# Attention, convolution and MLP layers on one core: where the convolution's taps stand in the attention, and which block goes first

## The chip, the cores and the metric

The kernel runs on one core of a Trainium2 chip, with all arithmetic in fp32. The metric is the device time of the execution in microseconds (us), the median of several runs. A profile, taken by the hardware from a further execution, gives every instruction of every engine: TensorE (PE, with weight loads as PEld), VectorE (DVE), ScalarE (ACT), GpSimd (POOL) and SyncE (SP), which issues the transfers (DMA).

## The reference

Four layers follow each other on x of 16 images, 384 channels, 16 x 16 pixels. Cut to what matters:

```
# layer 0: attention over 8 frames x 256 pixels (N = 2048 tokens), 12 heads of 32, batch of 2
q, k = xt @ qk_w.T ;  v = xt
attn = alpha * eye + beta * softmax(q k^T / sqrt(32)) - gamma / N
x = attn @ v
# layer 1: depthwise 7x7, LayerNorm over channels, MLP 384 -> 1536 -> 384
y = LN(conv7x7(x)) ; h = gelu(y @ w1 + b1)
h = grn_g * h * norm(h) / mean(norm(h)) + grn_b + h      # response normalization
x = x + h @ w2 + b2
# layer 2: x + gelu(LN(fusion_w @ [sobel_x(x), sobel_y(x)]))
# layer 3: 1x1, depthwise 3x3, 1x1 (with residual); linear attention; LN and MLP (with residual)
```

Layer 0 needs all tokens of a batch element. From layer 1 on, two images (512 columns) can be worked on by themselves.

## The kernel before

**Tiling.** Channels lie on partitions in three chunks of 128. The 2048 tokens of a batch element are four blocks of 512 columns; with two batch elements there are eight blocks, named here by (batch, block): (0, 0) is the first, (0, 1) the second.

**Attention (`attention`, L411).** The outer loop has six units (batch element, channel chunk of four heads), each with four blocks of queries, each with 16 steps over keys (`NQC` = 16). So there are 24 blocks of 16 steps, counted t = 0 to 383. A step has four score products (`st`) on TensorE, four exponentials (`e`) on ScalarE, and, a step later, four products with the values (`av`). The denominator needs the sum of e over all keys. VectorE adds the e of several steps into `s` (2048 elements a partition), and TensorE multiplies the group's sum with ones (`dn`). `ADDS` has the group size for each block: 16 means 15 sums on VectorE and one dn at the end; 4 means 12 sums, and the first three groups go to TensorE in four parts each. At a block's end a `finish` sends the denominator through DRAM twice (`away`, `few`, `back`, `r`) so that its reciprocal is cheap, and scales the result (`va`, `l`). Projections of q and k for the coming blocks (`p`) stand at the head of each block as long as there are any; the last stand at t = 320 and t = 336.

**Work put into the attention.** The attention's instructions are issued in a fixed order on PE, ACT and DVE (`InOrder`, L91). At each step `fill` (L1521) may put in operations of layer 1: the taps of the 7x7 convolution (`convolutions`, L906: per chunk one ScalarE pass and 48 multiply-adds on VectorE, rows y<-l,vec,y), and the *leads*, the normalization of the first two blocks (`layer1`, L1052). `pace` (L199) gives, for a step, how long TensorE is taken to need and how much VectorE has to do; the difference, less what was owed before (`lag`), is `free`. A VectorE operation is put in while `free` covers it. `FIRST` and `LEAD` are the first steps at which taps and leads may start. An operation that needs another ScalarE table (the square root of the normalization) is put in only ahead of a projection. Chunks listed together in `todo` alternate their taps; a chunk by itself runs its taps one after another, each dependent on the last. A chunk can start when the attention has finished that chunk of channels. The first matmul of the MLP waits for weights, and so can't stand in the attention.

**After the attention.** A planner (`Plan.all`, L185) orders all other operations from costs: at each turn it takes, of the operations that could start within `SLACK` of the earliest, the one whose task has the lowest rank (`RANK`: `mid` is layers 2 and 3 up to the linear attention, `l1` layer 1, `l3c` the last MLP, `conv` the remaining taps). `plan.level` (L1582) has VectorE begin 8 us and ScalarE 5 us after TensorE. `TURNS` is the order in which blocks use the MLP weights: each group loads its weights once and its first half may start only when the one before is through. `AFTER` says which block must have gone through layer 3's attention before the convolution of later blocks takes its tiles. Nearly every instruction is recorded with line L101, the helper that fixes the order, so the profile is read by the names of tiles: `ph_l` and `po_l` are the first and second product of layer 1's MLP, `ph_l3c` and `po_l3c` of the last, `su`, `sv` the products with ones for mean and variance, `s_l` their work tiles, `pg_l` the response normalization's, `pf_l` and `pc_l3a` those of layers 2 and 3.

Of the kernel before, what the change touches and what calls it, by code (L numbers as in the profile page):

```python
# [30 lines left out]
NIP = NBLK  # L31
NQC = N // P
PAIRED = (NB * NC - 1) * NBLK + 1
LEAD = 20 * NQC + 6
FIRST = NQC + 10

TURNS = (
# [1 line left out]
    (1, ((0, 0),)),  # L39
    (0, ((0, 3),)),  # L40
    (1, ((0, 1),)),
    (0, ((1, 0), (1, 1),)),
    (1, ((0, 2),)),
    (0, ((1, 3),)),
    (1, ((0, 3),)),
    (0, ((1, 2),)),
    (1, ((1, 1), (1, 0), (1, 3), (1, 2),)),
)
AFTER = ('x4', 0, 1)

RANK = {
    "mid": ((32.4, 40.6, 83.5, 47.6), (47.3, 49.0, 49.8, 34.6)),
    "l1": ((19.3, 43.7, 53.1, 86.8), (70.6, 16.2, 22.5, 90.5)),
    "l3c": ((87.9, 30.5, 79.2, 72.6), (54.9, 50.0, 67.3, 77.0)),
    "conv": 110.8,
}
SLACK = 0.191
JUNK = 2

ADDS = (16, 4, 16, 8, 8, 8, 16, 16, 4, 16, 8, 16, 4, 16, 8, 16, 16, 4, 16, 16, 16, 8, 16, 4)  # L60
XB, YB, SB = 12, 2, 22
TB = BLK // P
RB = 2 * HW
# [135 lines left out]
def pace(t):  # L199


    n, i = divmod(t - 1, NQC)
    adds = ADDS[n]
    pe, dve = 2.075, 2.2 if t and i % adds else 0.0
    parts = sum(
        min(k + 2 + j * adds // 4, NQC - 1) == i
        for k in range(adds - 1, NQC - 1, adds)
        for j in range(4)
    )
    pe += 0.21 * parts  # L210
    if i == adds + 1 and parts:
        pe += 0.15
    if t and i == NQC - 1 and n < PAIRED:
        pe += 1.1
    elif i == 1 and n > PAIRED:
        pe += 1.67
    elif not parts and adds < NQC and i > adds:
        pe += 0.09
    if n > 0:
        dve += {2: 0.17, 6: 0.6, 7: 0.66}.get(  # L220
            i - 2 * (n > PAIRED), 0.0
        )
    return pe, dve


class Task:
# [184 lines left out]
def attention(tc, X, xt, L0, block, small, col, cols, ones, load_qk, banks, fill, bound):  # L411
# [6 lines left out]
    with ExitStack() as actx:  # L418
# [50 lines left out]
        def unit(u, made, gm):  # L469

            b, g = units[u]
            q, keys, v = made["q"], made["k"], made["v"]
            adds = ADDS[u * NBLK : (u + 1) * NBLK]
            acc = {}
# [170 lines left out]
def conv_seq_kernel(  # L645
# [25 lines left out]
    def block(name, tag="x"):  # L671
        return blocks.tile([P, NC, BLK], F32, tag=tag, name=name, bufs=XB if tag == "x" else YB)
# [28 lines left out]
    def col(name, c, k=0):  # L701
        at, n = _COL[name]
        return vec[:, at + c * n + k : at + c * n + k + 1]
# [42 lines left out]
    pe, act, dve = (InOrder(tc, e) for e in (nc.tensor, nc.scalar, nc.vector))  # L746
# [149 lines left out]
    def together(*parts):  # L896

        parts = [[next(p), p] for p in parts]
        while parts:
            for p in list(parts):  # L900
                yield p[0]
                p[0] = next(p[1], None)
                if p[0] is None:
                    parts.remove(p)

    def convolutions():  # L906

        todo = [[(0, 0, 0)], [(0, 1, 0)], [(0, 0, 1)], [(0, 0, 2), (0, 1, 1)], [(0, 1, 2)]]
        todo += [[(b, i, c) for c in range(NC)] for b in range(NB) for i in range(NBLK)][YB:]
        for chunks in todo:  # L910
            for b, i, c in chunks:
                if c == 0:
                    tag = "y" if b == 0 or i < YB else "x"
                    after = [] if tag == "y" else [AFTER]
                    yield Op(None, 0.0, after=after, takes=[(tag, 1)], lag=0.0)
                    Y[b, i] = block(f"y_{b}_{i}", tag)
            yield from together(
                *(
                    depthwise(
                        Y[b, i][:, c, :],  # L920
                        L0[b][i][:, c, :],
                        lambda k, c=c: col("L1_dw_w", c, k),
                        col("L1_dw_b", c),
                        7,
                        ("y", b, i, c),
                        after=[("l0", b, i, c)],
                    )
                    for b, i, c in chunks
                )
            )  # L930
# [565 lines left out]

    bias = Task("bias", 0, fusion_bias())
    conv = Task("conv", RANK["conv"], convolutions())

    def rank(kind, b, i):  # L1500
# [12 lines left out]
    leads = [next(t for t in tasks if t.name == f"l1_0_{i}") for i in range(YB)]  # L1513

    if fast:
        open_pool("s", SB)
        open_pool("tiny", 2)

        lag = 0.0

        def fill(t, added=0.0):  # L1521


            nonlocal lag
            if t < 0:
                while plan.step(bias):
                    pass
                return
            if added is None:
                for task in leads:  # L1530
                    if task.head.table:
                        plan.step(task)
                return
            if t % NQC == 9 and t > NQC:
                u, i = divmod(t // NQC - 1, NBLK)
                plan.mark(("l0", u // NC, i, u % NC))
            length, work = pace(t)
            free = length + added - work - lag
            for task in (*leads, conv):
                if task.rest > t or t < (FIRST if task is conv else LEAD):  # L1540
                    continue
                before = None
                while task is not conv or ("y", 0, YB - 1, NC - 1) not in plan.made:
                    op = task.head
                    if op.table:
                        break
                    if before and before.engine != op.engine:
                        task.rest = t + 1 + (before.engine == "DVE")
                        break
                    if op.engine == "DVE":  # L1550
                        bank = any(tag == "mm" for tag, _ in op.gives)
                        if free < max(0.4, op.length - 1.5) and not bank:
                            break
                        free -= op.length + 0.12 * (before in op.after)
                    if not plan.holds(task, "wa") or not plan.step(task):
                        break
                    if op.engine in ("ACT", "PE"):
                        before = op
                        if task.head.engine == "ACT" and task is not conv:
                            task.rest = t + 1  # L1560
                            break
                    elif op.engine:
                        before = op
            lag = max(0.0, -free)

        attention(
            tc, X, xt, L0, block, small, col, cols, ones, first_loads, banks, fill, bound
        )
    else:
        attention_general(tc, X, L0, block, col, cols, ident, first_loads)  # L1570
        open_pool("s", SB)
        open_pool("tiny", 2)
# [33 lines left out]
    if fast:  # L1606
        tasks.append(Task("safety", 99, safety()))
    plan.all(tasks, SLACK)

# [90 lines left out]
```

## Time and profile before

| what | value |
|---|---|
| median of 3 runs | 2685.53 us (2685.33 to 2685.53) |
| the profiled execution's own time | 2687.06 us |
| its span, first to last instruction | 2685.1 us |
| PE busy | 2621.9 us (98%) |
| DVE busy | 2016.1 us (75%) |
| ACT busy | 1603.2 us (60%) |
| POOL busy | 7.5 us |
| granted TensorE clock, mean | 0.991 |
| end of the attention's last product on PE | 1033.5 us |
| DMA | 81.32 MB, 10% of the engines' time at most of the span |

The page has the span in 40 slices of 67.1 us, with a digit per slice for the busy tenths of each engine. A group's row has the operation, output <- input by the program's names, partitions x elements, the count, then busy time and mean of one, then the idle time before it and what ended it. A matmul in fp32 is recorded as two instructions, so that 72 rows of `po_l` are 36 products. A row in order of time has start, length, operation, and in brackets how long the engine had been idle before it and which operation ended that. In the slices 0 to 15 the attention runs, from slice 16 on the layers behind it.

### The profile page before, as it was taken

How to read it: one execution, taken by the hardware profiler on the slowest of the kernel's cores; microseconds unless marked ns; L12 is line 12 of the kernel's file. 1: busy time of each engine (PE TensorE's matmuls, PEld its weight loads, DVE VectorE, ACT ScalarE, POOL GpSimd, SP SyncE). 2: the span in 40 equal slices, each digit the busy share in tenths (PEclk: the TensorE clock that was granted, in tenths of full speed). 3: DMA queues.
4: the chain of work that ended last, by engine and by line, in shares of the span. 5: the costliest groups of instructions: out<-in, count | busy, mean ns of one | idle time of the engine just before them, and what ended most of it. 6: DMA issues, size and time to landing. Idle time of an engine off the chain costs nothing. (4 is left out here: it accounts for less than half of the span.)

```text
span 2685.1 us, 30687 instructions
## 1 busy us (share of the span) xinstructions
PE 2621.9 (98%) x11845; PEld 1026.3 (38%) x11845; DVE 2016.1 (75%) x2249; ACT 1603.2 (60%) x3083; POOL 7.5 (0%) x54
## 2 busy tenths in 40 slices
PE   9999999999999996899999999999999999999999
PEld 2222222222232222344444454445444544454443
DVE  5899999999999997999999899999653032542210
ACT  6888888888888895563554463654336644333220
POOL 0000000000000000000000000000000000000000
PEclk9999999999999998899999999999999999999999
DMA  3000000000000004000111112010110112000000
GB/s 142 18 9 21 6 17 17 9 21 6 17 17 5 9 17 138 0 1 0 36 36 36 53 57 79 24 36 12 36 59 24 35 59 94 12 1 12 1 12 25
DMA packets 51691, 81.32 MB, mean 30 GB/s; under 512 B 10608, under 2 KB 29168, under 8 KB 51536
## 3 DMA queue, kind: packets, MB, share of 16 engines
q1 hardware_dynamic: 51392, 79.12, 9.3%
q8 instruction: 95, 1.56, 0.2%
q14 instruction: 60, 0.49, 0.1%
q10 hardware_dynamic: 144, 0.15, 0.0%
HBM read 72.57 MB, written 6.68 MB: 30 GB/s over the span
## 5 line engine op out<-in xcount | busy, mean ns | idle before, releaser
L101 ACT ACTIVATE e<-st 128x512 f32<-128x512 f32 x1536 | 792.2, 611 | 56.3 <-PE st L101 36.7
L101 DVE TENSOR_TENSOR s<-s,e 128x2048 f32<-128x2048 f32 x294 | 673.6, 2291 | 26.9 <-ACT e L101 3.6
L101 DVE SCALAR_TENSOR_TENSOR y<-l,vec,y 128x420 f32<-128x420 f32 (+8 forms) x1152 | 660.6, 633 | 7.6 <-ACT y L101 1.4
L101 PE MATMUL st<-q,k 32*128 32x512 f32 x3072 | 451.2, 642 | 1.6 <-DVE y L101 1.3
L101 PE MATMUL av<-e,v 128*32 128x512 f32 x3072 | 437.2, 606 | 0.0
L101 PE MATMUL ph_l<-y,wa 128*128 128x512 f32 x576 | 260.4, 596 | 20.3 <-ACT y L101 20.3
L101 PE MATMUL po_l<-hid_l,wb 128*128 128x512 f32 x576 | 260.8, 601 | 2.3 <-ACT hid_l L101 2.2
L101 PE MATMUL ph_l3c<-d_l3c,wa 128*128 128x512 f32 x576 | 259.6, 595 | 0.0
L101 PE MATMUL po_l3c<-hid_l3c,wb 128*128 128x512 f32 x576 | 256.3, 593 | 0.0
L101 PEld LDWEIGHTS st<-q,k 32*128 32x128 f32 x3072 | 128.9, 183 | 285.2 <-issue 251.3
L101 PEld LDWEIGHTS av<-e,v 128*32 128x32 f32 x3072 | 79.8, 108 | 300.2 <-issue 274.5
L101 ACT ACTIVATE hid_l3c<-ph_l3c,vec 128x512 f32<-128x512 f32 x96 | 65.8, 686 | 190.2 <-PE ph_l3c L101 189.8
L101 ACT ACTIVATE hid_l<-ph_l,vec 128x512 f32<-128x512 f32 x96 | 65.8, 686 | 175.7 <-PE ph_l L101 175.6
L101 PEld LDWEIGHTS ph_l<-y,wa 128*128 128x128 f32 x576 | 109.6, 191 | 158.1 <-issue 126.8
L101 PEld LDWEIGHTS po_l<-hid_l,wb 128*128 128x128 f32 x576 | 109.2, 192 | 137.1 <-issue 122.9
L101 PEld LDWEIGHTS po_l3c<-hid_l3c,wb 128*128 128x128 f32 x576 | 109.0, 190 | 135.3 <-issue 133.2
L101 PEld LDWEIGHTS ph_l3c<-d_l3c,wa 128*128 128x128 f32 x576 | 108.1, 190 | 136.1 <-issue 129.5
L101 DVE SCALAR_TENSOR_TENSOR o_l3c<-po_l3c,vec,l 128x512 f32<-128x512 f32 x24 | 17.9, 748 | 187.4 <-PE po_l3c L101 186.6
L101 DVE SCALAR_TENSOR_TENSOR g_l3a<-h_l3a,dw,g_l3a 128x450 f32<-128x450 f32 (+1 forms) x192 | 119.2, 694 | 19.8 <-ACT g_l3a L101 19.7
L101 PE MATMUL p<-x,wqk_sb 128*128 128x512 f32 x288 | 131.2, 606 | 1.2 <-DMA x<-in_x_dram 1.2
L101 DVE TENSOR_TENSOR s<-e,e 128x2048 f32<-128x2048 f32 x45 | 102.9, 2286 | 35.1 <-ACT e L101 32.1
L101 ACT ACT_TABLE_LOAD x88 | 112.9, 1283 | 8.2 <-PE ph_l L101 4.5
(155 smaller groups left out, 2224.0 us busy)
## 6 DMA issues: line engine op xcount, KB each, us to landing
wa<-in_w_dram SPq DMA_DIRECT2D x15, 768.0 KB, 4.6
wb<-in_w_dram SPq DMA_DIRECT2D x15, 768.0 KB, 4.4
wa<-in_mlp_w_dram SPq DMA_DIRECT2D x15, 768.0 KB, 4.4
wb<-in_mlp_w_dram SPq DMA_DIRECT2D x15, 768.0 KB, 4.4
x<-in_x_dram SPq DMA_DIRECT2D x8, 768.0 KB, 9.3
v<-in_xt_dram SPq DMA_DIRECT2D x24, 256.0 KB, 10.7
r<-back SPq DMA_DIRECT2D x96, 64.0 KB, 2.1
out_dram<-o_l3c SPq DMA_DIRECT2D x24, 256.0 KB, 2.3
```

Of the source, the lines that this page charges most:

```text
L101: self.last = self.tc.keep_in_program_order(make(*args, **kw))
```

## The change

Four things are changed in the order of the work; no operation is added to the computation or left out.

- `pace` has other step lengths: 2.125 us for a step of TensorE in place of 2.075, 3.6 us for a block's last step, 0.16 us for a part of a group's dn.
- A tap is put in when `free` is at least 0.4 us and when VectorE, by `pace`, will not lag by more than 2.5 us at any step up to the block's end (new function `ahead`). Before, an operation needed `free` of its length less 1.5 us, and at least 0.4.
- The first block's second chunk in `todo` no longer alternates with the second block's: (0, 0, 2) stands by itself, then (0, 1, 1) and (0, 1, 2) alternate. The first block's lead may start at t = 294, the second's at 326 as before.
- `ADDS`, `TURNS`, `AFTER`, `RANK` and `SLACK` have other values.

```diff
-LEAD = 20 * NQC + 6
+LEAD = (18 * NQC + 6, 20 * NQC + 6)
...
-    (0, ((1, 0), (1, 1),)),
-    (1, ((0, 2),)),
-    (0, ((1, 3),)),
-    (1, ((0, 3),)),
-    (0, ((1, 2),)),
+    (0, ((1, 0),)),
+    (1, ((0, 2), (0, 3),)),
+    (0, ((1, 1), (1, 3), (1, 2),)),
     (1, ((1, 1), (1, 0), (1, 3), (1, 2),)),
 )
-AFTER = ('x4', 0, 1)
+AFTER = ('x4', 0, 2)
...
-    "mid": ((32.4, 40.6, 83.5, 47.6), (47.3, 49.0, 49.8, 34.6)),
-    "l1": ((19.3, 43.7, 53.1, 86.8), (70.6, 16.2, 22.5, 90.5)),
-    "l3c": ((87.9, 30.5, 79.2, 72.6), (54.9, 50.0, 67.3, 77.0)),
-    "conv": 110.8,
+    "mid": ((-10.7, 39.8, 15.4, 29.4), (92.4, 85.3, 93.3, 89.6)),
+    "l1": ((22.3, 22.5, 52.0, 45.4), (57.2, 52.1, 90.7, 8.2)),
+    "l3c": ((79.3, 2.7, 59.3, 70.1), (66.1, 61.4, 69.0, 118.4)),
+    "conv": 80.5,
 }
-SLACK = 0.191
+SLACK = 0.122
...
-ADDS = (16, 4, 16, 8, 8, 8, 16, 16, 4, 16, 8, 16, 4, 16, 8, 16, 16, 4, 16, 16, 16, 8, 16, 4)
+ADDS = (16, 8, 8, 16, 16, 16, 8, 8, 8, 4, 8, 8, 16, 4, 8, 4, 8, 8, 4, 8, 16, 16, 16, 16)
...
-    pe, dve = 2.075, 2.2 if t and i % adds else 0.0
+    pe, dve = 2.125, 2.2 if t and i % adds else 0.0
...
-    pe += 0.21 * parts
-    if i == adds + 1 and parts:
-        pe += 0.15
     if t and i == NQC - 1 and n < PAIRED:
-        pe += 1.1
+        pe = 3.6
     elif i == 1 and n > PAIRED:
         pe += 1.67
-    elif not parts and adds < NQC and i > adds:
-        pe += 0.09
+    elif parts:
+        pe += 0.16 * parts + 0.2 * (i == adds + 1)
...
+def ahead(t):
+
+    worst = gain = 0.0
+    while (t + 1) % NQC:
+        t += 1
+        pe, dve = pace(t)
+        gain += pe - dve
+        worst = min(worst, gain)
+    return worst
...
-        todo = [[(0, 0, 0)], [(0, 1, 0)], [(0, 0, 1)], [(0, 0, 2), (0, 1, 1)], [(0, 1, 2)]]
+        todo = [[(0, 0, 0)], [(0, 1, 0)], [(0, 0, 1)], [(0, 0, 2)], [(0, 1, 1), (0, 1, 2)]]
...
-            for task in (*leads, conv):
-                if task.rest > t or t < (FIRST if task is conv else LEAD):
+            for task, start in zip((*leads, conv), (*LEAD, FIRST)):
+                if task.rest > t or t < start:
...
-                        if free < max(0.4, op.length - 1.5) and not bank:
+                        left = free - op.length
+                        if (free < 0.4 or left + ahead(t) < -2.5) and not bank:
                             break
```

## The prediction

> **What bounds the kernel now.** I read the forty slices first, then TensorE's waits, then the trace around the longest wait, then one block of the attention.
>
> ```profile
> PE   9999999999999996899999999999999999999999
> DVE  5899999999999997999999899999653032542210
> PEclk9999999999999998899999999999999999999999
> ```
>
> TensorE (PE) is full everywhere but in slices 16 and 17, where the attention ends; there alone the granted clock falls too. VectorE (DVE) is just as full until slice 28, so two engines share the bound over the first 1,880 us, and only after that TensorE alone. TensorE's own waits, whole kernel:
>
> ```profile
> PE ph_l L101 <- ACT y L101: 20.3, 1, 20.3
> PE dn L101 <- DVE s L101: 14.2, 14, 3.6
> PE pg_l L101 <- DVE gs_l L101: 3.2, 3, 1.9
> PE su_l L101 <- DVE s_l L101: 3.2, 1, 3.2
> PE sv_l L101 <- DVE s_l L101: 2.8, 2, 2.0
> ```
>
> One wait of 20.3 us is a third of all TensorE idle time (2685.1 - 2621.9 = 63.2 us). In order of time, TensorE:
>
> ```profile
> 1032.50 1.06 PE L101 MATMUL dn<-s,ones 128*32 128x512 f32 x8 [0.99 <-DVE s L101]
> 1053.91 9.69 PE L101 MATMUL ph_l<-y,wa 128*128 128x512 f32 x18 [20.35 <-ACT y L101]
> 1091.95 2.05 PE L101 MATMUL su_l<-s_l,ones 128*128 128x512 f32 x2 [3.17 <-DVE s_l L101]
> 1100.69 33.36 PE L101 MATMUL po_l<-hid_l,wb 128*128 128x512 f32 x72
> ```
>
> and VectorE over the same time:
>
> ```profile
> 1039.64 0.25 DVE L101 RECIPROCAL few<-few 128x16 f32<-128x16 f32 x1 [7.20 <-DMA few<-away]
> 1046.41 0.69 DVE L101 TENSOR_TENSOR va<-va,r 128x512 f32<-128x512 f32 x1 [6.51 <-DMA r<-back]
> 1047.87 3.34 DVE L101 RECIPROCAL s_l<-s_l 128x512 f32<-128x512 f32 x1
> 1051.25 1.76 DVE L101 TENSOR_TENSOR y<-y,s_l 128x1536 f32<-128x1536 f32 x1
> ```
>
> The first MLP matmul needs the normalised first block. Its square root was done by 1042.2, but its reciprocal stands in VectorE's queue behind the last block's reciprocal and scaling, which wait for two round trips through DRAM (7.20 and 6.51 us idle). So TensorE stands from 1033.5 to 1053.9. Last, a block of the attention with 16 sums in a row:
>
> ```profile
> 810.22 19.05 DVE L101 TENSOR_TENSOR s<-s,e 128x2048 f32<-128x2048 f32 x8
> 829.19 5.04 DVE L101 SCALAR_TENSOR_TENSOR y<-l,vec,y 128x390 f32<-128x390 f32 x9
> 829.33 1.07 PE L101 MATMUL dn<-s,ones 128*32 128x512 f32 x8 [1.03 <-DVE s L101]
> ```
>
> Dependent sums start 19.05/8 = 2.38 us apart, while an unhindered TensorE step takes 2.07 (st starts at 745.95 and 748.02). VectorE sets the pace here, and TensorE waits for the last sum before dn.
>
> [...] The trace has 2291, so the kernel's 2.2 is low whenever the next sum depends on it. [...] clock 0.50 from 1038 to 1054, and 9.69 us for nine ph products against 23.42/27 = 0.87 us for later ones. [...]
>
> **The change, part by part.**
>
> *What goes into the attention.* I added up the placement rule's own numbers step by step, only for where an operation stands. For the kernel before this gives 243 taps in the attention: five chunks of 48 and 3 of the sixth. The trace agrees: 245 up to 1053.6, of which two start after 1052.9. One block shows the sum: 15 x 2.075 + 3.175 of steps and 5.4 of projections is 39.7; less 15 x 2.2 + 1.43 of VectorE work, 5.3 remains, or 8 taps at 0.66. After: 15 x 2.125 + 3.6 + 5.4 - 34.4 = 6.4, or 10 taps. The end-of-block test hardly refuses a tap: from a block's first step on, even a 16-sum block lacks only 14 x 0.075 + 1.43 - 2.125 = 0.36 of the 2.5 us of lag that it allows. Over 24 blocks with the new group sizes: 256 taps, all 144 of the first block and 64 of the second's. So the first block's lead may begin at step 294; the rule puts its mean at 300, its variance at 307 and its square root at 320, the next projection, with reciprocal and multiply behind and the affine at 322 to 324. Nothing of it is left for the attention's end.
>
> *Cost of that.* VectorE, attention only: sums 339 to 337, -2 x 2.29 = -4.6. Taps: alone they cost 8.63/13 = 0.66 (13 at 109.51), two chunks in turn 8.73/15 = 0.58 (783.92). Before, 147 x 0.66 + 96 x 0.58 = 152.7; after, 192 x 0.66 + 64 x 0.58 = 163.8: +11.1. Reciprocal and multiply move in: 3.35 + 1.76 = +5.1. Sum +11.6. VectorE was idle for only 13 us in the attention (7 of it before 98 us, in a block that now takes more sums), so about 4 of this finds room: **+8 us** (bounds 0, if the 3.61 us wait at 870 with its half clock to 877 goes too, and +13). It is not certain that VectorE sets every block, hence the lower bound.
> TensorE: groups that close within a block rise from 21 to 23, eight more parts at 0.33 us = 2.6 us, covered by VectorE's pace; without that cover they cost their 2.6. ScalarE: two table loads of 1283 ns and a square root of 0.69 at step 320, 3.3 us beside a 2.7 us projection; ScalarE is 61.9 of 67 us full there at worst, so I take nothing, at most 3.
>
> *The attention's end.* From dn's end (1033.5) to the first po (1100.7) are now 67.2 us. After: 36 ph products at 0.87 = 31[...]. The first weight chunk was issued at 1003.81, the second at 1034.95, 4.9 us to landing, and is wanted 10 us after the end, so DMA is hidden. ScalarE stands at the last block's check till 6.7 us after the end; GELU and squares (1.93 a chunk against 2.6) catch up. Then the response norm: from ph's end at 1088.8 to po at 1100.7 took 11.9 now[...]. No other product is ready then but su and sv of the second block, so the wait stays, and VectorE, still blocked for 14 us at the end where the order assumes 8, makes it some 13. Together 44: **-23 us** (bounds -27 and -17).
>
> *Behind it.* From po to the end are 1584.4 us, with 7.6 us of waits. The second block still lacks 16 taps on each of two chunks: 32 x 0.58 = 19 us, then 8 us of weight preparation and 16 of mean, variance and reciprocal from VectorE's release at 14: ready 57 us after the end, before po is through at 75. But against po's start it is 8 us later than before (there multiplied at 1105.6, 5 after po; then 13), and the next feed is just in time. I take **+5 us** (bounds -6, the new priorities removing waits, and +30). Twelve MLP loads fewer (30+30 to 24+24): hidden, as DMA is 10% busy.
>
> Sum: 8 - 23 + 5 = -10. The span goes from 2685.1 to 2675, the profiled execution's own 2687.06 to 2677, and the shown median of 2685.53, 0.4 above the span, to **2675.5 us**. The late priorities and turn groups (RANK, TURNS, SLACK, AFTER) are otherwise costed at zero: VectorE falls to 6 tenths at 1,880 us while TensorE has 800 us of work left, so late order has cover; if it had none, each tenth of a slice is 6.7 us.
>
> **Rivals.** *Fed throughout* (0.22): the attention grows by 2 only, since blocks bound by TensorE take the taps, and the early order keeps it fed: 2 - 27 - 4 = -29, 2657. For it: tap cost is spread over more groups of 8 and 4; against: from dn to dn nearly every block now takes 41 to 43 us, whatever its group size, as where VectorE sets it.
> *Given back* (0.18): VectorE is full to 1,880 us, so what TensorE does early it waits for later, at pc or po between 1,180 and 1,350 where waits of 0.8 to 2.3 us already show. The gain of 23 goes in equal parts to the longer attention and to these: 2685. Against: after 1,350 VectorE is ahead of need by most of a block's taps.
> *Slower* (0.22): the first block's middle layers, now first in rank, push back the third block's 144 taps. After the second block VectorE has 80 us of taps, 45 for each of two middles (10.6 of edges, 14.8 of 3x3 taps, two reciprocals of 3.35, the rest from the rows at 1176 to 1293) and 16 to normalise: with 57, ready at 243 after the end. TensorE has cover to about 44 + 31 + 31 + 31 + 72 + 60 = 269 (MLP halves of 36 products; a middle of 54 at 0.86, 24 at 0.65 and 10 us of small ones). The margin is 26; if the middles' chained waits stretch VectorE's list by more than 26 + 15 us, it is slower, each further us costing one. At 25 beyond[...], 2702.
> That the change does nothing at the end (square root not reached by 336) is within *given back*; its variance at step 307 leaves 13 steps to the projection at 320 and 29 to that at 336.
>
> **How the numbers follow.** Forecast 0.38, the three rivals 0.22, 0.18, 0.22. About 0.2% (5.4 us) is what a measurement here can tell. Faster: 0.22, most of the forecast (0.34) and a little of the third: 0.57. Within: 0.19. Slower: 0.24. The forecast's own range is 2665 to 2685; to hold 8 in 10 I leave out the ends of the fast and slow cases: 2655 to 2702.
>
> **What would show it.** Right: ph_l follows dn within a microsecond at the attention's end, near 1041 us; sqrt and a 128x512 reciprocal near 870 to 890; 256 taps before the end; a wait of 8 to 13 us before the first po. Wrong: dn waits of more than 1 us in most blocks (attention longer than 1046), waits of PE for DVE over 15 us in total between 1,100 and 1,500, or a new wait after 1,900.

## The result, and the profile after

The change made the kernel slower: 2699.39 us (median of 5 runs, 2698.93 to 2701.21) against 2685.53 (median of 5, 2685.33 to 2690.25) for the kernel before in the same measurement. Over all ten runs the ratio is 1.0046, with a 95% interval of 1.0031 to 1.0061. The forecast was 2675.5. The profiled execution's own time is 2698.93 us, its span 2697.1.

Blocks of the attention are numbered 0 to 23 here, as in `ADDS`; block n is steps 16n to 16n + 15, and its time runs from the start of the last `dn` of block n - 1 to that of its own. The stretches that the forecast used, in us:

| stretch | before | after | difference | forecast |
|---|---|---|---|---|
| start to the end of the last dn | 1033.5 | 1052.5 | +19.0 | +8 |
| from there to the first po | 67.2 | 57.2 | -10.0 | -23 |
| first po to the end | 1584.4 | 1587.4 | +3.0 | +5 |
| span | 2685.1 | 2697.1 | +12.0 | -10 |

So two of three terms failed, both in the same direction. In the forty slices of the kernel after (one digit per slice, the busy tenths):

```profile
PE   9999999999999998799999999999999999999999
DVE  5899999999999997899999795697962445252020
PEclk9999999999999999899999999999999999999999
```

TensorE's dip at the attention's end (slices 15 and 16, counted from 0; the prediction counts them as 16 and 17) reads 8 and 7 where it read 6 and 8. VectorE has slices of 5 to 7 tenths from slice 22 on, before only from slice 28 on. TensorE's waits over the whole kernel (total, times, longest):

```profile
PE dn L99 <- DVE s L99: 16.8, 13, 6.4
PE po_l L99 <- ACT hid_l L99: 12.0, 4, 5.4
PE su_l L99 <- DVE s_l L99: 10.2, 1, 10.2
...
PE st L99 <- DVE y L99: 2.7, 1, 2.7
PE pg_l L99 <- DVE gs_l L99: 2.5, 2, 1.9
```

The 20.3 us wait for the normalised block is gone. In its place stand a wait of 10.2 us of `su` (the product for the second block's mean), one of 5.4 of `po`, and one of 6.4 at the last `dn`. TensorE in order of time, from the last block on:

```profile
1050.58 1.94 PE L99 MATMUL dn<-s,ones 128*32 128x512 f32 x8 [6.38 <-DVE s L99]
1052.45 22.04 PE L99 MATMUL ph_l<-y,wa 128*128 128x512 f32 x48
...
1077.06 5.40 PE L99 MATMUL ph_l<-y,wa 128*128 128x512 f32 x12
1092.62 2.05 PE L99 MATMUL su_l<-s_l,ones 128*128 128x512 f32 x2 [10.17 <-DVE s_l L99]
1094.46 5.99 PE L99 MATMUL ph_l<-y,wa 128*128 128x512 f32 x12
...
1103.94 0.38 PE L99 MATMUL pg_l<-gs_l,ones 128*128 128x2 f32 x2 [1.95 <-DVE gs_l L99]
1109.70 2.92 PE L99 MATMUL po_l<-hid_l,wb 128*128 128x512 f32 x3 [5.38 <-ACT hid_l L99]
```

`ph_l` starts with dn's end. But after 30 of its 36 products (60 rows) `su` is next in TensorE's queue, and the six products behind it, which could have run, wait with it. What `su` waits for is in VectorE's queue, in order of time:

```profile
1058.86 0.25 DVE L99 RECIPROCAL few<-few 128x16 f32<-128x16 f32 x1 [8.34 <-DMA few<-away]
1065.33 0.69 DVE L99 TENSOR_TENSOR va<-va,r 128x512 f32<-128x512 f32 x1 [6.21 <-DMA r<-back]
...
1066.79 12.45 DVE L99 SCALAR_TENSOR_TENSOR y<-l,vec,y 128x420 f32<-128x420 f32 x23
...
1086.35 4.80 DVE L99 SCALAR_TENSOR_TENSOR y<-l,vec,y 128x390 f32<-128x390 f32 x9
...
1091.78 0.69 DVE L99 TENSOR_TENSOR s_l<-s_l,y 128x512 f32<-128x512 f32 x1
```

VectorE is held by the last block's two round trips through DRAM until 1066.8, 14.3 us after the attention's end; then it owes 32 taps, with 7 us of weight preparation between them.

The longer attention. Single blocks, in us:

| kernel | blocks 1-17 | block 18 | blocks 19-21 | blocks 22-23 | sum |
|---|---|---|---|---|---|
| before | 716.4 | 41.8 | 126.0 | 77.1 | 961.4 |
| after | 727.0 | 49.5 | 127.3 | 75.3 | 979.1 |

And VectorE in that time, from 72 us to the start of the last `dn` (columns: stretch, its length, VectorE's busy time and instructions, granted TensorE clock, DMA share, GB/s), before and then after:

```profile
72.00:1032.50 960.50, 917.39 (x643) 0.99 0.05 14
```

```profile
72.00:1050.58 978.58, 929.49 (x656) 1.00 0.05 14
```

VectorE's work grew by 12.1 us, its idle time from 43.1 to 49.1. The step from work to time is where the forecast went wrong: it expected 4 of the 11.6 us of new work to find room, and instead 6 us of new idle came on top. (The forecast's 13 us of idle time were waits alone. In before, VectorE's waits of more than 0.15 us come to 17.0 of the 43.1 us; the rest are short pauses, most of them ahead of a sum.) Block 18 alone, where the first block's mean now stands, is 7.7 us longer. Of the +19.0, 17.6 us are in this table, 0.4 lie ahead of block 1, and 0.9 is the last `dn` itself, 1.94 us after its long wait where it took 1.06.

### The profile page after: what moved, and what is told of

It is laid out like the page before. It is cut to its first block, busy times and chain, and to the rows that moved or that the text cites. A ratio compares the mean times of both kernels' runs of the same rounds, so it can differ in the third digit from the quotient of the medians.

```text
span 2697.1 us, 30768 instructions
## 1 busy us (share of the span) xinstructions
PE 2635.4 (98%) x11909; PEld 1035.5 (38%) x11909; DVE 2010.6 (75%) x2247; ACT 1582.0 (59%) x3069; POOL 7.4 (0%) x54
## 4 chain that ended last, share of the span: by engine, by line
PE 76%; DVE 20%; issue 2%; ACT 2%; DMA 0%; DVEq 0%; SPq 0%
DVE s L99 12%; PE po_l L99 9%; PE st L99 9%; PE po_l3c L99 9%; PE ph_l3c L99 9%; PE av L99 8%; PE ph_l L99 6%; PE pf_l L99 5%; DVE y L99 4%; PE p L99 3%; PE pk_l3b L99 2%; PE pv_l3b L99 2%; PE pq_l3b L99 2%; PE pp_l3b L99 2%; PE pc_l3a L99 2%
## 5 line engine op out<-in xcount | busy, mean ns | idle before, releaser
L99 DVE TENSOR_TENSOR s<-s,e 128x2048 f32<-128x2048 f32 x290 | 664.4, 2291 | 27.7 <-ACT e L99 3.8
L99 PE MATMUL st<-q,k 32*128 32x512 f32 x3072 | 458.7, 641 | 2.9 <-DVE y L99 2.7
L99 PEld LDWEIGHTS st<-q,k 32*128 32x128 f32 x3072 | 135.4, 183 | 283.3 <-issue 245.6
L99 ACT ACTIVATE hid_l<-ph_l,vec 128x512 f32<-128x512 f32 x96 | 65.8, 685 | 170.7 <-PE ph_l L99 170.3
L99 ACT ACTIVATE hid_l<-hid_l,vec,gx_l 128x256 f32<-128x256 f32 x192 | 104.6, 615 | 10.3 <-DVE gx_l L99 10.1
```

The source lines that it names most:

```text
L99: self.last = self.tc.keep_in_program_order(make(*args, **kw))
```

## The experiments

Two things were to be explained, the +18 of the attention and the 13 us missing at its end, and behind both stood a third: how much of each comparison is only the late order (`RANK`, `SLACK`) fitting one placement of the taps. All ratios are to the kernel before, measured in the same session on the same chip (medians 2686.93 to 2687.84).

### The end: when VectorE is free

```diff
-    plan.level({"DVE": 8.0, "ACT": 5.0})
+    plan.level({"DVE": 14.4, "ACT": 6.7})
```

> Changed kernel with one number pair other: the order behind the attention is planned with VectorE free 14.4 us and ScalarE 6.7 us after the attention's end (measured there), in place of 8 and 5. In TensorE's queue the second block's mean product (su) then stands behind all 36 first products of the first block, not behind 30 of them. Theory A (the gain at the attention's end was half lost because su waits 10.2 us with six products of ph behind it): attention as before within 1 us (last dn near 1050.6), the wait of su gone or under 4 us, first po near 1100 in place of 1109.7, total 8 to 11 us below the changed kernel. Theory B (VectorE bounds the first part behind the attention, so TensorE waits later for what it gets earlier): po earlier as well, but the total within 3 us of the changed kernel.

Measured: 2692.28 us, ratio 1.0019 (1.0010 to 1.0029), about 7 us below after (8 to 11 were expected). TensorE in order of time in this kernel:

```profile
1054.74 21.95 PE L99 MATMUL ph_l<-y,wa 128*128 128x512 f32 x48
...
1079.23 10.55 PE L99 MATMUL ph_l<-y,wa 128*128 128x512 f32 x24
1095.23 2.05 PE L99 MATMUL su_l<-s_l,ones 128*128 128x512 f32 x2 [5.45 <-DVE s_l L99]
```

With the true time of VectorE's release the planner puts all 36 `ph` products ahead of `su`, whose wait falls from 10.17 to 5.45 us (under 4 was expected), and from dn's end to po are 49.2 us in place of 57.2. So 8 of the 13 us that the forecast missed come from an order planned for engines that are free too early, VectorE by 6.4 us; ScalarE's number was changed together with it and not by itself. What is left is a wait as the forecast had it, until the second block's 32 taps are done.

### The lead: taken out, moved, given another block

```diff
-LEAD = (18 * NQC + 6, 20 * NQC + 6)
+LEAD = (24 * NQC, 24 * NQC)
```

> Changed kernel with no normalization inside the attention (both leads barred there); 273 taps in place of 256 go in. Theory A: block 18 of the attention falls from 49.5 us to about 43, the attention ends 2 to 6 us earlier than 1052 (7.7 + 5.1 less, 17 taps of 0.6 more). The wait of ph for the normalized first block comes back, over 25 us; but both blocks' ph then run in one piece, so that the wait before po (16 us in the changed kernel) goes. Total within 6 us of the changed kernel. Theory B: the same total within 3 us, with waits of PE for DVE between 1150 and 1400 moved but not fewer. If the lead was a plain gain of 20 us, the total is 15 to 20 us above the changed kernel.

Measured: 2744.81 us, ratio 1.0211 (1.0194 to 1.0228). The expectation of the total missed: behind the attention this order, made for a lead that is done, waits for it (`su` 17.4 and 10.8 us). The attention is the part to read; it ends 8 us earlier, where 2 to 6 were expected. Blocks 1 to 17 take 727.1 us (727.0 in after), block 18 takes 42.9 in place of 49.5, blocks 19 to 21 take 125.8 in place of 127.3. VectorE over the attention of this kernel:

```profile
72.00:1042.58 970.58, 929.32 (x666) 1.00 0.05 14
```

The rule fills the lead's place with 17 more taps, so that VectorE does the same work as in after, 929.3 against 929.5 us, and yet the attention is 8 us shorter. The lead's price there isn't its VectorE time; it is 8 us in which VectorE stands, 4.3 of them in block 18 and 3.9 in blocks 19 to 21. What happens is seen in 6 us of block 18, in after and then in this kernel (busy time and instructions of PE, PE's loads, VectorE, ScalarE, POOL, then the clock):

```profile
831.00:837.00 6.00, 5.50 (x34) 1.64 (x38) 3.36 (x3) 1.03 (x2) 0.00 (x0) 0.72 0.00 0
```

```profile
831.00:837.00 6.00, 6.00 (x74) 2.15 (x65) 5.80 (x5) 5.51 (x12) 0.00 (x0) 1.00 0.01 4
```

In the first, the kernel after, TensorE issues 34 instructions in place of 74 at 0.72 of the clock, and ScalarE has 2 in place of 12. The events around it in the kernel after, TensorE and then VectorE in order of time:

```profile
831.50 1.12 PE L99 MATMUL st<-q,k 32*128 32x512 f32 x2 [2.66 <-DVE y L99]
```

```profile
829.69 1.75 DVE L99 SCALAR_TENSOR_TENSOR y<-su_l,y 128x1536 f32<-128x1536 f32 x1
...
834.66 2.29 DVE L99 TENSOR_TENSOR s<-e,e 128x2048 f32<-128x2048 f32 x1 [2.59 <-PE dn L99]
838.67 2.29 DVE L99 TENSOR_TENSOR s<-s,e 128x2048 f32<-128x2048 f32 x1 [1.71 <-ACT e L99]
```

The score product waits 2.66 us until VectorE has subtracted the mean (`su_l` and the scores share PSUM banks); then TensorE is late, at a lower clock (the 0.72 above), ScalarE has no scores to work on, and VectorE waits for TensorE's and ScalarE's output in turn. The next experiment tries whether VectorE being late is the cause, by starting the lead a block earlier:

```diff
-LEAD = (18 * NQC + 6, 20 * NQC + 6)
+LEAD = (17 * NQC + 6, 20 * NQC + 6)
```

> Changed kernel with one number other: the first block's lead may start at step 278 in place of 294. Its sums then fall to the head of block 18 (steps 0 to 3, where VectorE owes nothing) in place of steps 9 to 12 (where it lags); 256 taps and the order behind the attention stay as they are. Theory A (block 18 takes 7 us too long because a score product waits for the bank of the lead's mean, which the lagging VectorE reads late, and TensorE then runs at half clock): block 18 from 49.5 to 44 us or less, the wait of st for VectorE gone or under 0.5 us, the attention ends 4 to 7 us earlier, total 4 to 7 us below the changed kernel. Rival (the lead's VectorE work itself, about 9 us, costs the time): block 18 and 19 together as before within 2 us, total unchanged.

Measured: 2698.39 us, 1.0040 (1.0025 to 1.0055), so nothing of it came. TensorE's wait, in order of time, fell to 0.89 us:

```profile
810.86 1.13 PE L99 MATMUL st<-q,k 32*128 32x512 f32 x4 [0.89 <-DVE y L99]
```

and yet block 18 takes 49.5 us again, with a clock of 0.73 from 812 to 818. A shorter wait did not make the block shorter, so theory A failed. But the block's work isn't the same: the product `sv` for the variance, 1.1 us, which stands in block 19 in after (855.4), now stands in block 18 as well (828.6). So this run doesn't tell how much of the 6.6 us the wait is. Blocks 18 and 19 together take 91.0 us against 91.3, as the rival had it; its cause, the lead's VectorE work itself, does not fit the run without the lead, where the same amount of VectorE work took 8 us less. What both kernels have in common is that the mean meets block 18, which is summed in groups of four. So the block was changed instead:

```diff
-ADDS = (16, 8, 8, 16, 16, 16, 8, 8, 8, 4, 8, 8, 16, 4, 8, 4, 8, 8, 4, 8, 16, 16, 16, 16)
+ADDS = (16, 8, 8, 16, 16, 16, 8, 8, 8, 4, 8, 8, 16, 4, 8, 4, 8, 8, 16, 8, 16, 16, 16, 16)
```

> After, with block 18, in which the first block's mean stands, summed in one group of 16 in place of groups of 4; the rule then places 243 taps (256 in after), the mean in block 18 or 19, the square root still in the attention. In after block 18 takes 49.5 us, without the lead 42.9. Theory A (the 6.6 us are the price of the lead in a block that TensorE sets: its two products and a wait for VectorE with half the clock behind it come on top of TensorE's work; where 15 dependent sums set the block, TensorE has room): blocks 18 to 21, 176.8 us in after, take 171 to 174, no block of them over 45, and the last dn begins at 1045 to 1048. Theory B (the lead costs 7 to 8 wherever it stands, VectorE's 4.5 us included): one block still takes 48 or more, and the last dn begins at 1049 to 1053. Both: the late order is fitted to 256 taps, so the total is no test; 2690 to 2760.

Measured: blocks 18 to 21 take 170.7 us (176.8 in after), block 18 takes 43.1, no block over 43.2, and the last `dn` begins at 1044.75. VectorE over the attention, in the columns used above:

```profile
72.00:1044.75 972.75, 928.78 (x646) 1.00 0.05 14
```

Its work is 0.7 us less than in after, its idle time 44.0 in place of 49.1. Theory A holds, a little below both of its ranges: with a single group of 16 in that block the attention is 2.2 us longer than with no lead at all. The mean's sums now fall at the very end of block 18, and its `su` at the head of block 19 (847.1), which is in groups of 8. So this is a lead behind a block of 16 sums, not in one; and since no run has block 18 in one group of 16 without the lead, the 2.2 us hold the change of groups too. At the head of block 19 `st` again waits, 1.77 us, but the clock from 854 to 860 is 1.00 and VectorE is busy for 5.79 of these 6 us. The reading is that it has a store of finished `e` to sum, since 15 dependent sums had kept it behind TensorE, and that in groups of four it had caught up with TensorE, so that each stall of one was a stall of both. This fits these four runs, and is not shown by itself. The total, 2775.96 us (1.0331, 1.0314 to 1.0348), is no test, as said ahead: from po to the end it is 1673.0 us.

### The taps: step lengths, placement and groups

After with the step lengths and the placement test of before:

```diff
-    pe, dve = 2.125, 2.2 if t and i % adds else 0.0
+    pe, dve = 2.075, 2.2 if t and i % adds else 0.0
...
-                        left = free - op.length
-                        if (free < 0.4 or left + ahead(t) < -2.5) and not bank:
+                        if free < max(0.4, op.length - 1.5) and not bank:
```

> Changed kernel with the old placement rule and old step lengths (2.075, 0.21 a part, no look ahead), all else as changed: 221 taps in place of 256, the first block's normalization still inside. Theory A (in the attention VectorE sets the pace, so each tap there costs its 0.6 us): 35 taps less are 21 us of VectorE, the attention ends 12 to 20 us earlier, near 1036. Behind it 35 more taps stand before the second block, so a part comes back: total 5 to 12 us below the changed kernel. Theory B: all of it comes back, the total is that of the changed kernel within 3 us. Rival C (TensorE sets the pace in the attention): the attention ends within 4 us of 1052.

Measured: 2711.47 us, 1.0088 (1.0072 to 1.0105). 221 taps stand in the attention, 35 fewer, and the last `dn` begins at 1038.60, 12 us earlier, as theory A had it: 6.9 of it in blocks 1 to 17, 2.4 in block 18. A tap of 0.64 us costs the attention 0.34 on the average. The total, which theory A had 5 to 12 us below after, went the other way: from po to the end 1616.8 us, 29 more than after.

This run also bears on the lead. The mean stands in block 18, as in after. Block 18 by itself (the stretch, its length, then the columns of the 6 us views):

```profile
791.51:838.54 47.03, 45.99 (x375) 14.63 (x375) 38.28 (x31) 38.20 (x76) 0.00 (x0) 1.00 0.06 18
```

The clock is 1.00 throughout, VectorE is idle for 8.8 us, `st` waits 1.04 us, and still the block takes 4.1 us more than without the lead. So the low clock is not needed for the larger part of the lead's price in this block, nor a VectorE that is behind.

Then after with the group sizes of before:

```diff
-ADDS = (16, 8, 8, 16, 16, 16, 8, 8, 8, 4, 8, 8, 16, 4, 8, 4, 8, 8, 4, 8, 16, 16, 16, 16)
+ADDS = (16, 4, 16, 8, 8, 8, 16, 16, 4, 16, 8, 16, 4, 16, 8, 16, 16, 4, 16, 16, 16, 8, 16, 4)
```

> After, with the group sizes (ADDS) of before alone; the rule then places 237 taps in the attention, the first block's lead stays in it (mean in the last block but five, square root behind the projection after). Theory A (the attention grew by its placement: the lead 8 us, the rest from the choice of groups together with the taps that they let in): before had 243 taps and no lead and its last dn began at 1032.5; 237 taps at about 0.3 us each less, the lead's 8 more, so the last dn begins at 1037 to 1041. Theory B (the added taps of the new step lengths are what costs, group sizes don't matter): 19 taps less than after at 0.3 to 0.6 are 6 to 11 us, so it begins at 1040 to 1045, and a block with the same sums as before takes more than before wherever it has more taps. Both: the time from po to the end isn't that of after, because the late order is fitted to 256 taps; total anywhere from 2690 to 2770.

And before with the first block's convolution and lead ahead of the second's alone:

```diff
-LEAD = 20 * NQC + 6
+LEAD = (18 * NQC + 6, 20 * NQC + 6)
...
-        todo = [[(0, 0, 0)], [(0, 1, 0)], [(0, 0, 1)], [(0, 0, 2), (0, 1, 1)], [(0, 1, 2)]]
+        todo = [[(0, 0, 0)], [(0, 1, 0)], [(0, 0, 1)], [(0, 0, 2)], [(0, 1, 1), (0, 1, 2)]]
```

> Before, with the first block's convolution and lead ahead of the second's alone (todo and LEAD of the change; step lengths, placement test, group sizes, ranks of before): 224 taps in the attention. Theory A (the lead costs about 8 us of attention wherever it stands, taps 0.3 us each): 8 - 19 x 0.3 = +2, the last dn begins at 1034 to 1036. Rival (the lead is nearly free where the last blocks have groups of 4 and 8, and its cost in after came from the groups of 16): the last dn begins at 1026 to 1029. Both: the 20.3 us wait for the normalised block goes, and a wait of su for the second block's last taps comes, as VectorE is released 14 us after the attention's end; 32 more taps of the second block stand behind the attention, which the late order of before doesn't expect: total 2680 to 2750.

| kernel | taps in the attention | blocks 1-17 | block 18 | blocks 19-21 | blocks 22-23 | median, ratio (95%) |
|---|---|---|---|---|---|---|
| before with new `todo` and `LEAD` | 224 | 715.8 | 41.6 | 129.9 | 72.5 | 2710.51, 1.0088 (1.0071-1.0105) |
| after with old groups | 237 | 722.6 | 41.8 | 131.3 | 72.1 | 2703.99, 1.0063 (1.0046-1.0079) |

The last `dn` of after with old groups begins at 1039.69, where theory A put it, 0.3 us short of theory B's range. That of the other begins at 1031.37, between the two expectations, so both missed; and the wait for the normalised block did not go (20.98 us), because with the old rule and the old groups together the variance product runs at 920.06, after the last place at which a table may change. Either the new rule (in this pair) or the new groups (in the run ahead of it) brings the lead through in time.

What they tell together. In blocks 1 to 17 the four kernels with the new `todo` make a square:

| blocks 1-17 | step lengths and test of before | of after |
|---|---|---|
| groups of before | 715.8 us, 192 taps | 722.6 us, 200 taps |
| groups of after | 720.1 us, 192 taps | 727.0 us, 214 taps |

The new groups cost 4.3 us without a single tap more (4.4 under the new rule), although VectorE is busy 4.4 us less in them, 680.6 in place of 685.0. They give TensorE eight more parts of `dn` there, which the forecast priced at 2.6 us and took for covered; what the other 1.7 us are isn't shown. The new rule costs 6.8 and 6.9 us, with 8 taps more under the old groups and 22 under the new ones, so it isn't one price per tap. Block by block under the old groups: nine more taps, in six blocks with groups of 8 or 16, took 6.2 us, 0.7 each, their full length; four more in a block with groups of four took 0.2; five fewer in three other blocks gave nothing back. Under the new groups too, five more in three blocks of 16 took 3.6 us, and seven more in three blocks of four 1.3. The order of the chunks matters as well: before, where two chunks take turns from block 14 on, holds 203 taps in 716.4 us, 11 more than with the new `todo` in nearly the same time.

The lead. Before had paid for its mean and variance in blocks 22 and 23 already: 77.1 us, against 72.5 when they stand earlier; after should have gained those 4.6, and gives 2.6 of them back to the last block's single group of 16, as the next run shows. Nor is a lead cheap in every block of 16 sums. With the old groups the mean stands in block 19, which is one group of 16, and blocks 18 to 21 take 3.7 and 5.2 us more than in before, with 15 and 11 taps fewer.

### The late order

After with the last block in groups of four:

```diff
-ADDS = (16, 8, 8, 16, 16, 16, 8, 8, 8, 4, 8, 8, 16, 4, 8, 4, 8, 8, 4, 8, 16, 16, 16, 16)
+ADDS = (16, 8, 8, 16, 16, 16, 8, 8, 8, 4, 8, 8, 16, 4, 8, 4, 8, 8, 4, 8, 16, 16, 16, 4)
```

> Changed kernel with the attention's last block in groups of 4 in place of 16, as in the kernel before: 12 sums in place of 15, and 9 taps more go in. Theory A (at the end VectorE's lag counts as such): the wait of 6.4 us of the last dn goes to about 1 us, but three groups' dn parts (12 x 0.33 us) and the taps take its place, so the attention ends within 3 us of 1052 and the total is within 4 us of the changed kernel. Rival (the wait is plain loss): attention 5 us shorter and total 5 us lower.

Measured: the last block takes 35.0 us in place of 37.6, with 9 taps more in the attention, as theory A had it. But where it expected a total within 4 us of after, the kernel takes 2771.97 us, 1.0315 (1.0298 to 1.0332), as from po to the end it takes 1662.8. The three longest of TensorE's waits behind the attention, in that kernel:

```profile
PE ph_l3c L99 <- ACT d_l3c L99: 17.6, 3, 8.7
...
PE sv_l3c L99 <- DVE s_l3c L99: 11.8, 3, 6.2
PE pc_l3a L99 <- DVE l L99: 9.4, 3, 4.7
```

They are in layer 3. The thought was that nine taps that are no longer there make the same ranks give another order for everything behind. So the ranks were chosen anew, by a search with the planner's own costs, for four kernels; each also has the true release of VectorE and ScalarE (14.4 and 6.7). First before itself:

```diff
-SLACK = 0.191
+SLACK = 0.126
...
-    plan.level({"DVE": 8.0, "ACT": 5.0})
+    plan.level({"DVE": 14.4, "ACT": 6.7})
```

(and all of `RANK`)

> Kernel before, with nothing of the change but new numbers for the order behind the attention: VectorE released 14.4 us and ScalarE 6.7 us after the end as measured, and ranks searched anew for that. Attention and the wait of 20 us at its end stay. Theory A (the order behind the attention was already good; the release alone moves a few products): total within 6 us of the kernel before. Rival (most of what the later runs gain is a better order, open to the kernel before as well): 8 us or more below the kernel before.

Measured: 2683.74 us, 0.9986 (0.9980 to 0.9993), within theory A's 6 us. The attention is as in before, and from po to the end it takes 1579.6 us in place of 1584.4. Then after with the last block in groups of four and the lead from step 278:

```diff
-LEAD = (18 * NQC + 6, 20 * NQC + 6)
+LEAD = (17 * NQC + 6, 20 * NQC + 6)
...
-SLACK = 0.122
+SLACK = 0.129
```

(with the last entry of `ADDS` 4, the release, and all of `RANK`)

> Changed kernel with the lead at step 278, the last block in groups of 4, the measured release (14.4 and 6.7 us) and ranks searched anew for this placement; taps in the attention 265. Theory A (the 72 us that the last block's group size cost before came from ranks that fit one placement of taps only; the group size itself saves 2 to 3 us): attention ends 6 to 9 us before that of the changed kernel, near 1044; from the first po to the end 1575 to 1590 us as in the two given kernels, not 1663; total 2673 to 2683. Theory B (with the last block of 4 something else is late behind the attention): from po to the end over 1620 us.

Measured: 2683.46 us, 0.9987 (0.9981 to 0.9994). With 265 taps placed as in the run of 1662.8 (the lead a few steps earlier), from po to the end it is now 1586.0. So the 77 us were the order's (the release, changed with the ranks, was worth 7 us of after's total), not the placement's. The attention ends at 1048.1, not near 1044, and the total is just above the expected range. Then the same with the old step lengths and placement test (231 taps), ranks of its own and `SLACK` 0.097:

> As e7 (lead at step 278, last block in groups of 4, measured release, ranks searched anew), but with the old placement rule: 231 taps in the attention in place of 265. Theory A (a tap inside the attention costs about 0.3 us of its length, behind it less than that once the order fits): attention ends 10 us before that of e7, near 1034 as in the kernel before, with the first block still normalized inside; from there to the end 4 to 8 us more than e7; total 2666 to 2676, below the kernel before. Theory B (taps left over cost behind the attention what they cost inside): total as e7 within 3 us. Theory C (they cost more behind, as e3 seemed to say): 10 us or more above e7.

Measured: 2677.78 us, 0.9967 (0.9955 to 0.9979), faster than both kernels, just above the expected 2666 to 2676. Against the one above, the attention is 12.3 us shorter and the time behind po 5.5 longer (1591.5). TensorE at the attention's end:

```profile
1034.76 1.06 PE L99 MATMUL dn<-s,ones 128*32 128x512 f32 x8 [1.47 <-DVE s L99]
1035.76 20.87 PE L99 MATMUL ph_l<-y,wa 128*128 128x512 f32 x48
...
1082.27 12.20 PE L99 MATMUL po_l<-hid_l,wb 128*128 128x512 f32 x24 [3.73 <-ACT hid_l L99]
```

From dn's end to po are 46.5 us, and `su` stands behind 12 products of po. Block 18, in groups of four with the whole of the mean and variance in it, still takes 47.1 us there. Hence the last run, that kernel with block 18 in one group of 16, 217 taps, ranks of its own and `SLACK` 0.181:

```diff
-ADDS = (16, 8, 8, 16, 16, 16, 8, 8, 8, 4, 8, 8, 16, 4, 8, 4, 8, 8, 4, 8, 16, 16, 16, 4)
+ADDS = (16, 8, 8, 16, 16, 16, 8, 8, 8, 4, 8, 8, 16, 4, 8, 4, 8, 8, 16, 8, 16, 16, 16, 4)
...
+    "mid": ((4.8, 73.2, 87.6, 55.9), (120.0, 70.6, 116.6, -43.6)),
+    "l1": ((100.7, 35.5, 11.1, 76.5), (118.3, 115.1, 107.4, 31.0)),
+    "l3c": ((34.8, 148.3, -8.4, -141.4), (-11.8, 47.3, -15.9, 13.4)),
+    "conv": 370.1,
```

> The kernel of fewer taps (old step lengths and placement rule, ranks of its own), with block 18 summed in one group of 16 in place of groups of 4, 217 taps in the attention, and RANK and SLACK chosen anew for that. Theory A (the lead is cheap in a block of 16 sums, and a late order chosen for its own placement costs nothing): block 18 takes 42 to 44 us instead of 47.1, the last dn begins at 1029 to 1032 instead of 1034.8, from the first po to the end stays within 1580 to 1595, and the total is 2668 to 2676, faster than both kernels and than the kernel of fewer taps. Rival (14 taps more behind the attention take back what it gains: VectorE feeds TensorE late behind po): from po to the end over 1597, total 2677 to 2690.

Measured: 2670.57 us, 0.9936 (0.9922 to 0.9949), the fastest of all, 15 to 17 us below before, 13 below before with its own searched order, and 29 below after. Block 18 takes 43.5 us, as theory A had it, but the attention as a whole is only 1.2 us shorter (962.0 against 963.3), since the other blocks, block 20 above all, give 2.3 of the 3.5 us back, and the last `dn` begins at 1033.94, later than expected. The other 6 us are behind po: 1585.3 against 1591.5. So the part of theory A that this run confirms is the total and the block; that a shorter attention makes the gain is only in small part true. Against before, the gain lies where the forecast of the change had put it: from dn's end to po it is 47.9 us in place of 67.2 (44 was forecast), with an attention as long as before's. TensorE, in order of time, at the attention's end of this kernel:

```profile
1033.94 1.06 PE L99 MATMUL dn<-s,ones 128*32 128x512 f32 x8 [1.58 <-DVE s L99]
1034.93 20.87 PE L99 MATMUL ph_l<-y,wa 128*128 128x512 f32 x48
...
1082.89 17.36 PE L99 MATMUL po_l<-hid_l,wb 128*128 128x512 f32 x36 [3.85 <-ACT hid_l L99]
```

## Why the prediction was wrong

**What held.** The placement: 256 taps, 337 sums, the lead through before the attention's end (VectorE's reciprocal at 890.47). VectorE's added work: +11.6 worked out, +12.1 measured. The removed wait: 20.35 us, and `ph` right behind `dn`. The term behind po: +5 worked out, +3.0 measured.

**"About 4 of this finds room: +8 us": failed, by 11 us.** This took VectorE's idle time for a store that new work can draw on, and VectorE for the engine that sets every block, so that TensorE's new parts were "covered by VectorE's pace". Measured were +19.0 us; 1.3 of it lie ahead of block 1 and in the last `dn`, the rest in three places.

- Blocks 1 to 17, +10.6 us. The new groups cost 4.3 at an equal number of taps and with less VectorE work, so TensorE's parts were not covered. The new rule costs 6.9 more; under the old groups a tap that is added to a block with groups of 8 or 16 costs its full length (6.2 us for nine), in groups of four nearly nothing (0.2 us for four). The new `todo` takes off 0.6, with 11 taps fewer.
- Block 18, +7.7 us. The lead's products stood in the attention before too, so the forecast put no price on their new place. With equal VectorE work the lead costs 8 us where it was put, in groups of four, most of it in this block, and about 2 us behind a block of 16 sums: by the reading given above, a new dependence between the two engines (TensorE's scores wait for the lead's mean) makes both stand.
- Blocks 19 to 23, -0.5 us: before's own lead in blocks 22 and 23, 4.6 us, goes, and a last block in one group of 16 and the rest of the new lead take nearly all of it back.

The upper bound of 13 that the forecast gave for this term was too low, as it was VectorE's work with no cover and left out that work can also cost more than its length, here 12.1 us of it with 6 us of new idle time on top.

**"No other product is ready then but su and sv of the second block, so the wait stays": failed, by 13 us.** A wait was foreseen, of some 13 us; 10.2, 1.95 and 5.4 us were measured. Its place was not foreseen. The forecast had all 36 `ph` products run first and the wait begin behind them; in TensorE's queue `su` stands ahead of the last six, since the planner had VectorE free 8 us after the attention's end. The forecast named that difference, 14 against 8, as a lengthening of the last wait, and did not ask which products the planner would queue behind `su` because of it. With the level corrected the stretch took 49.2 us, where 44 was forecast; the remaining 5 us were not taken apart.

**The late order, "otherwise costed at zero".** In this change it did cost nothing, +3.0 behind po, but that was luck. The reason given, that VectorE's low load gives it cover, is wrong all the same: with VectorE as idle late as ever, 9 taps more and unchanged ranks cost 75 us there. The ranks of after happened to be made for its placement.

**The rivals.** *Fed throughout* had the attention 2 us longer, as blocks bound by TensorE take the taps; it is 19 us longer, and only groups of four took added taps at nearly nothing (0.2 us for four). *Given back* has the right mechanism in its first half, a gain that goes to a longer attention, at 2685 too small; its second half did not come: TensorE's waits at pc and po between 1,180 and 1,350 are 2.7 us in all, and were 5.0 before. *Slower* put the loss at the third block's taps, far behind the attention, where TensorE's waits for `pc` are these 2.7 us. The sign that the forecast itself named, an attention longer than 1046, came, but not by dn waits in most blocks (16.8 us in 13, against 14.2 in 14).

**What stays open.** Of the 6.6 us in block 18, the wait of 2.66, the 1.7 that the rows behind it take longer at the clock of 0.72 (`av` 1.57, `dn` 0.68 and `st` 2.06 us in place of 1.06, 0.40 and 1.14) and `su`'s 1.1 make 5.4; the rest isn't settled, nor how the 4.1 us at full clock in the run with the old rule are made up, nor what part VectorE's being level with TensorE in groups of four has in either. Nor is it shown how much of the two last kernels' gain a new search with the right release could have given to after itself, with its own groups and placement.

## What to carry to other kernels

Work that is put into another stage has to be priced per block by who waits in it, not by an engine's busy sum: the same 929 us of VectorE work took 971, 973 or 979 us here, by whether and where the lead stood between the sums and how they were grouped around it. A queue worked in order has to be asked what stands behind each new wait; a planner that thought VectorE free 6.4 us too early put six ready `ph` products behind `su`'s wait of 10.17 us here. And where an order is the outcome of a search for one placement, a part of a change can't be tried alone by total time: compare the stage, or search again, as with 2771.97 and 2683.46 us for nearly the same placement.

## What the runs showed of the hardware

- Blocks 1 to 17 took 727.0 or 727.1 us in all seven kernels that share their groups and step lengths, at a granted clock that read 1.00 over these blocks in after (72 to 798.5 us). Block 18 with one and the same order took 49.3, 49.5 and 50.6 us in three of them (last block in groups of four, after, release), and TensorE's rows behind the wait of 2.66 us in it took 1.6, 1.7 and 2.8 us more than the same rows (`st` 1.14, `av` 1.06, `dn` 0.40 us) before the wait.
- In the records of the granted clock of before and after, all eleven stretches at half the clock that end before the span does last 3.4 us or a multiple of it: 3.4, 6.8, 10.2, 13.7 or 20.5 us.
- The granted clock read 0.72 (after, 831 to 837) and 0.73 (the lead a block earlier, 812 to 818) over 6 us windows behind single waits of only 2.66 and 0.89 us, while waits of 1.77 us (one group of 16 in block 18) and 1.04 us (the old rule) left it at 1.00. So in these four the length of the wait alone does not tell whether the clock falls.
- In the last block of after, 15 sums of 2.29 us, those in a row 2.38 us apart (14.26 us for six), stand ahead of one `dn`: TensorE waited 6.38 us for the last sum there, as in four more kernels with 16 as the last group (release, no lead, the lead a block earlier, block 18 in one group of 16), and 0.99 to 2.07 us in before and in four kernels of the experiments with a last block in groups of four (the two of 265 taps, and those of 231 and 217). Here the size of the last group was a latency at the stage's end.
